# Layer 0's second dense layer goes through DRAM in 26 of 32 graphs, under new planner constants

## The chip, the cores and the metric

The kernel runs on one NeuronCore of a Trainium2 chip. The metric is device time in microseconds for one execution of the whole program, as the median of several runs. Five engines work side by side, each on its own queue of instructions in order: PE multiplies matrices and writes its results into eight banks of PSUM; DVE (VectorE) and ACT (ScalarE) work element by element and are the ones that read the banks; POOL (GpSimd) computes a few powers here; SP (SyncE) issues the transfers, which 16 DMA engines carry out.

## The reference

32 graphs, each with 512 nodes of 256 features and a weighted 512x512 adjacency, pass four layers. Every layer adds its result to its input and normalises each node over the 256 features.

```
x = ln(x + relu(((1+eps)*x + adj@x) @ W1 + b1) @ W2 + b2)          # layer 0, 256 -> 512 -> 256
x = ln(x + prelu(adj @ (x @ W.T + b)))                              # layer 1
h = ln'(x); x = ln(x + x + relu((adj@h)@W_rel + b_rel + h@W_root))  # layer 2
x = ln(x + silu(rms((eps*x + adj@x) @ W1 + b1)) @ W2 + b2)          # layer 3, 256 -> 1024 -> 256
```

Here `ln` is the plain layer norm, `ln'` the one with gain and offset, `rms` a norm over the 1024 hidden values. Everything is float32.

## The kernel before, in words

**Layout.** Within a graph, the 512 nodes are cut into four chunks of 128 (`NC = 4`); a tensor "by token" has the nodes on the 128 partitions, one "by feature" has the features there. All matrix products are made by a scheme of seven products for a 2x2 block product (`seven`, line 851): sums of blocks are formed first on DVE (`left_sums`, `right_sums`, `dense_sums`), seven smaller products go through three banks, and each result is taken out of its bank by a copy or an add.

**Layer 0's second dense layer** (in `layer0`): the hidden tensor h1 is by feature, the result must be by token, to be added to x. In the kernel before, `dense_add` (line 1072) does it in every graph. It uses h1's blocks as the stationary operand and W2's blocks (`A2_0`, 128 columns wide) as the moving one, so its matmuls are 128 columns wide, and the result is by token at once; `take` adds each bank to x on DVE. The bias row b2 has been added to x before (`plus_row`, two DVE adds of 128x512, with a broadcast load by `passing`).

**The other way**, `dense_turned` (line 1097), is used by layer 3 in graphs 1 to 28. It keeps the weights stationary and streams 256 columns of hidden values. The result yT is by feature, four of its evictions are made by ACT, which adds the bias at the same time (`act(..., bias=...)`), and it then has to be turned over: two DVE transposes turn every 32x32 square, and `spread_squares` (line 1277) moves the squares to their places by four stores to a DRAM tile and two loads back. `add_turned` adds the two halves to x on DVE and calls the half of the norm that follows. The DRAM tiles come from a ring of ten (`corners`), which layer 2's `gather_squares` uses as well.

**Which way** is decided by `turns(layer)` (line 1050) from the table `TURN` (line 140): `TURN[0] = (99, 0)` means never.

**Order of the work.** Nothing is issued in the order of the source. Every instruction is entered into a plan (`Plan`, line 286) with its modelled duration and its dependencies. `Plan.order` (line 484) then simulates the engines, picks at each step the op of lowest rank that can start, assigns rooms (35 buffers of 128x1024 in SBUF) and banks, and writes the order out. The rank of an op is its graph times a period, plus a shift of that graph (`SHIFT`), plus how late it may be (`needs`). Up to five graphs are in flight (`FLIGHT = 5`). Constants tell the planner what things cost: `LOAD`, `CORNER`, `TURNED` and the like are (time on the wire, time after it) of transfers, `SPARE` is a margin added to every landing, `HAND` the hand-over between engines, `YIELD` a penalty that keeps DVE from ops that ACT could do, `GENTLE` and `AHEAD` how early loads and ops of later graphs may start. An op with two ways, such as `copy` (line 743) or `Norm.put` (line 1215), goes to the engine that the planner finds sooner free.

**Ends.** The program begins with nine matmuls on zeros (line 1524) while the first loads come in. In the last two graphs (`HALVES = 2`) layer 3 uses `NormOnVector`: for each half of the nodes, once its `dense_add` is complete, DVE takes `bn_stats` of each chunk of 256 features and `bn_aggr` of it, and `finish` scales and stores that half.

```
def turns(layer):
    return TURN[layer][0] < plan.graph < B - TURN[layer][1]
...
if turn:
    add_turned(x, dense_turned(right, A2_0, b2c_0), norm.half)
else:
    dense_add(x, right, A2_0, norm.half)
```

Of the kernel before, what the change touches and what calls it, by code (L numbers as in the profile page):

```python
# [13 lines left out]
ALU = mybir.AluOpType  # L14

P = 128
# [5 lines left out]
def span(ap):  # L22

    n = 1
    for d in ap.shape[1:]:
        n *= d
    return n
# [5 lines left out]
def matmul_time(n):  # L33
    return (0.224 if n <= 128 else 0.432 * n / 256), 0.163
# [6 lines left out]
def vector_time(n):  # L41
    return 0.07 + n * 0.00104, 0.055 if n <= 256 else 0.08
# [7 lines left out]
def stats_time(n):  # L50
    return 0.095 + n * 0.00092, 0.082
# [22 lines left out]

SPARE = 1.2


KEEP = 0.4  # L80
# [3 lines left out]
    return 0.1 + kbytes / 450, 1.0  # L84


LOAD, LOAD_X, BLOCK = (0.86, 1.8), (0.67, 1.4), (0.3, 0.66)
KEPT, BACK = (0.31, 0.5), (0.33, 0.94)
CORNER, PIECES = (0.43, 0.84), (0.61, 1.09)
TURNED, QUARTER = (0.75, 1.05), (0.59, 1.05)  # L90
LINE, SPREAD, RESULT = (0.22, 0.1), (1.45, 0.83), (0.66, 1.1)

GENTLE = 3.5
LOADS = 2

HAND = dict(tensor=0.12, vector=0.09, scalar=0.09, gpsimd=0.14, sync=0.1)
WEIGHTS, AGAIN = 0.09, 0.09


# [13 lines left out]
SOON = 0.03  # L115


YIELD = 0.8

# [2 lines left out]

RULES = [(37, 1.65, 19, 0.9)]

SHIFT = {-1: -26, 0: 12, 1: 3, 2: 2, 5: -1, 7: 1, 14: -1, 29: -7, 30: -16, 31: 4}
HALVES = 2
AHEAD, LAST = 50.0, 500.0
TURN = {0:(99,0),2:(99,0),3:(0,3)}
ROWS = 1
ONE = 1
PLAIN = 0
# [148 lines left out]
class Plan:  # L286
# [191 lines left out]
    def best(self):  # L478


        rule = min(RULES, key=lambda rule: self.order(*rule)[0])
        return self.order(*rule)[1]

    def order(self, period, pace, last, near):
# [28 lines left out]
        while can_start:  # L513
# [52 lines left out]
            for i in can_start:  # L566
# [9 lines left out]
                if op.gentle:  # L576
                    wait = max(wait, wire - GENTLE)
                at = {
                    e: max(free[e] + BEFORE * (op.crosses and not crossed), wait, ready[i][e], port[e] if op.port else 0.0) for e in op.ways
                }  # L580
                way = min(
                    at, key=lambda e: at[e] + sum(op.ways[e][0]) + YIELD * (op.yields and op.graph < B - PLAIN and e == "vector")
                )
# [30 lines left out]
            if op.wire:  # L614
                wire = max(wire, t + ADVANCE) + op.wire
                end = wire + op.late + SPARE + LOADS * op.gentle
                if engine == "sync":
# [11 lines left out]
            for n, result, more in op.then:  # L629
                behind[n] -= 1  # L630
                for e in ready[n]:
                    if e != engine or e != "tensor" and result:
                        ready[n][e] = max(ready[n][e], end + HAND[e] + more)
                if not behind[n]:
# [12 lines left out]
def tile_gnn_stack(ctx: ExitStack, tc: tile.TileContext, a: dict, out: bass.AP):  # L647
# [26 lines left out]
    B, N, D = a["x"].shape  # L674
    NC = N // P
# [5 lines left out]
    HC = NC // 2  # L681
# [8 lines left out]
    plan = Plan(nc, FLIGHT)  # L690
# [31 lines left out]
    def vector(method, n, *args, **kw):  # L722
        return "vector", method, vector_time(n), args, kw
# [2 lines left out]
        columns = sum(k in ("scale", "bias") and not isinstance(v, float) for k, v in kw.items())  # L726
        return "scalar", "activation", times(n, columns), (x,), dict(func=func, **kw)

    def mm(o, lhsT, rhs, first, last):
        kw = dict(start=first, stop=last, skip_group_check=True)  # L730
        way = "tensor", "matmul", matmul_time(span(rhs)), (lhsT, rhs), kw
        plan.do(o, way, ordered=o.room)

    def flip(o, x):
# [20 lines left out]
    def ts(o, x, s1, s2, op0, op1=None):  # L755
        kw = dict(op0=op0) if op1 is None else dict(op0=op0, op1=op1)
        plan.do(o, vector("tensor_scalar", span(o), x, s1, s2, **kw))
# [22 lines left out]
    def small(*shape):  # L780
        return Part(Room(smalls)).shaped(*shape)
# [13 lines left out]
    def half(t, h):  # L795
        return t[:, h * HC : (h + 1) * HC]

    class Wide:


        def __init__(self, n):
            self.n = n
            self.rooms = [room(2, N) for _ in range(n // 2)]
# [245 lines left out]

    def turns(layer):  # L1050

        return TURN[layer][0] < plan.graph < B - TURN[layer][1]

    def halves(x):

# [13 lines left out]
                right.setdefault(m, []).extend(x[:, e] for e in range(n))  # L1069
        return right  # L1070

    def dense_add(x, right, left, done, kind="add"):


        def block(i, j):
            return x[:, j * HC : (j + 1) * HC, i * P : (i + 1) * P]

        def product(m, ps, first):
            n = len(right[m])
            for k in range(n):  # L1080
                for i in range(HC):
                    mm(
                        ps[:, i, :], right[m][k][:, i], left[m][:, k, :],
                        first and i == 0 and k == 0, k == n - 1,
                    )

        def take(ps, i, j):
            add(block(i, j), ps, block(i, j))

        def put(ps, i, j, more):  # L1090
            take(ps, i, j)
            if i == 1:
                done(j)

        seven(kind, partial(bank, HC, P), product, take, put)

# [73 lines left out]
    class Norm:  # L1170
# [33 lines left out]
        def finish(self, h, m, plus, place):  # L1204

            mine = slice(h * HC, (h + 1) * HC)
            ve, rstd, shift = self.ve[:, mine], self.rstd[:, mine], self.shift[:, mine]
            ts(ve, self.squares[:, mine], m / self.n, plus, ALU.mult, ALU.add)
            inv_sqrt(rstd, ve)
            mul(shift, self.less[:, mine], rstd)  # L1210
            for c in range(h * HC, (h + 1) * HC):
                self.put(c, self.r, rstd[:, c % HC : c % HC + 1], shift[:, c % HC : c % HC + 1])
            plan.move(place, half(self.r, h), RESULT, into=f"out{plan.graph}{h}")

        def put(self, c, y, scale, shift):
            r = self.r[:, c, :]
            plan.do(
                y[:, c, :],
                vector(
                    "tensor_scalar", D, r, self.less[:, c : c + 1], scale, op0=ALU.add, op1=ALU.mult  # L1220
                ),
                scalar(AF.Identity, D, r, scale=scale, bias=shift),
            )

# [9 lines left out]
    class NormOnVector(Norm):  # L1234


        def half(self, h):
            means = self.few.then(lambda v: v[:, 0 : 2 * NC].rearrange("p (c i) -> p c i", i=2))
            for c in range(h * HC, (h + 1) * HC):
                st = self.few[:, 8 + 6 * (c % HC) : 14 + 6 * (c % HC)]  # L1240
                plan.do(st, ("vector", "bn_stats", stats_time(D), (self.r[:, c, :],), {}))
                plan.do(means[:, c, :], ("vector", "bn_aggr", stats_time(6), (st,), {}))
            mine = slice(h * HC, (h + 1) * HC)
            ts(self.less[:, mine], means[:, mine, 0], -1.0, None, ALU.mult)
            self.squares, self.n = means[:, :, 1], 1
# [84 lines left out]
    def passing(name):  # L1330

        t = short(N)[:, 0:D]
        plan.move(t, a[name].partition_broadcast(P), D / 2)
        return t

    def plus_row(x, r):
# [138 lines left out]
    def layer3(x, adjacency, b):  # L1475

        aT = aggregate(x, adjacency)
        turn = turns(3)
        if not turn:
            plus_row(x, passing("L3_gnn_b2"))  # L1480
        hT, acc = Wide(FC3), short(N)

        def squares(f):
            sq = room(2, N)
            act(sq, hT.pair(f), AF.Square)
            if f == 0:
                add(acc, sq[:, 0, :], sq[:, 1, :])
            else:
                add(acc, acc, sq[:, 0, :])
                add(acc, acc, sq[:, 1, :])  # L1490

        dense_feat(aT, A1_3, b1_3, hT, squares)
        pr = everywhere(column_sums(acc), (1.0 / HID3, RMS_EPS, ALU.mult, ALU.add))
        right = {}
        for q in range(0, FH, 2):
            for f in (q, q + 1, FH + q, FH + q + 1):
                mul(hT.chunk(f), hT.chunk(f), pr)
                act(hT.chunk(f), hT.chunk(f), AF.Silu, scale=w_3[:, f : f + 1])
            for m, t in dense_sums([halves(hT.pair(q))], [halves(hT.pair(FH + q))]).items():
                right[m] = right.get(m, []) + t  # L1500
        norm = (NormOnVector if b == 0 or b >= B - HALVES else Norm)(x)
        place = out[b].rearrange("(p c) d -> p c d", c=NC)
        if b < B - HALVES:
            if turn:
                add_turned(x, dense_turned(right, A2_3, b2c_3), norm.half)
            else:
                dense_add(x, right, A2_3, norm.half)
            norm.scales((1.0, LN_EPS))
            y = norm.scaled()
            for h in range(2):  # L1510
                plan.move(half(place, h), half(y, h), RESULT, into=f"out{b}{h}", gentle=b < B - 4)
        else:

            def done(h):
                norm.half(h)
                norm.finish(h, 1.0, LN_EPS, half(place, h))

            dense_add(x, right, A2_3, done)

    plan.graph = -1
    idle, zeros = bank(D), scraps[0]
    for _ in range(9):
        mm(idle, zeros[:, 0:P], zeros, True, True)
    eps0 = row("L0_gnn_eps")
    one_eps0 = constant("one_eps0", [P, 1])
    ts(one_eps0, eps0, 1.0, None, ALU.add)
# [4 lines left out]
    x = load_x(0)  # L1533
# [14 lines left out]
    x = layer0(x, adjacency)  # L1548
# [9 lines left out]
    h = layer1(x, adjacency)  # L1558
# [9 lines left out]
    A2_3 = weight_sums("A2_3", *blocks_of(W2_3[:, 0:FH], W2_3[:, FH:]))  # L1568
    layer3(layer2(*h, adjacency), adjacency, 0)
    for b in range(1, B):  # L1570
        plan.graph = b
        x, adjacency = load_x(b), Adjacency(b)
        h = layer1(layer0(x, adjacency), adjacency)
# [45 lines left out]
```

## Time and profile before

| what | value |
|---|---|
| median of 3 runs | 2274.05 us (2273.98 to 2274.63) |
| the profiled execution | 2273.29 us, its span 2271.5 us |
| PE busy | 2260.4 us, 12806 matmul records |
| DVE busy | 2128.1 us (94%) |
| ACT busy | 1807.5 us (80%) |
| mean granted TensorE clock | 0.999 |
| moved by DMA | 172.00 MB, queue q1 26.3% of 16 engines' span |

The span runs from the first instruction to the last; the time of an execution holds a little around it. Each float32 matmul of the source stands as two records in the profile. Records of matmuls overlap their neighbours, so a busy PE is not yet a PE at its peak: the step from one start to the next tells what a matmul costs. Names are those of the program without buffer numbers: `room` is any of the SBUF buffers, `ps` a bank of PSUM, `few` a small buffer, `corner` a DRAM tile of the turning, `A` the sums of weight blocks. As one helper issues everything, nearly all instructions have the same line, and groups are told apart by their names and shapes. "Idle before, releaser" is the time for which an engine rested ahead of an instruction, and what ended the rest.

### The profile page before, as it was taken

What the parts mean: (1) busy time and instruction counts of PE and PEld (TensorE: products, weight loads), DVE (VectorE), ACT (ScalarE), POOL (GpSimd) and SP (SyncE); (2) the same over time, 40 slices, a digit from 0 to 9 for tenths busy, and PEclk for the clock granted to TensorE, in tenths of its full rate; (3) what the DMA queues carried; (4) which work ended last, traced back from release to release, by engine and by line L of the source; (5) the groups of instructions that cost most, each with busy time, mean ns of one, the idle gap of its engine ahead of it and who ended that gap; (6) DMA issues with size and microseconds to landing.
All of it is one profiled execution on the core that took longest, in us unless ns stands there. A gap on an engine that the chain in (4) does not pass through costs nothing.

```text
span 2271.5 us, 39581 instructions
## 1 busy us (share of the span) xinstructions
PE 2260.4 (100%) x12806; PEld 2041.0 (90%) x12806; DVE 2128.1 (94%) x5458; ACT 1807.5 (80%) x4981; POOL 243.5 (11%) x168
## 2 busy tenths in 40 slices
PE   9999999999999999999999999999999999999998
PEld 8889988999989999989999899998999989989888
DVE  8999999999999999989999999999999999999898
ACT  4877778787788787887788887879787788778686
POOL 0100110101011110111011010110111011101011
PEclk9999999999999999999999999999999999999999
DMA  7201331323332233322332313331231322232201
GB/s 220 62 17 34 87 96 42 101 58 93 84 77 54 75 92 89 93 54 67 85 90 61 100 44 90 89 93 51 73 117 52 88 75 53 77 91 48 75 22 59
DMA packets 261790, 172.00 MB, mean 76 GB/s; under 512 B 143824, under 2 KB 213456, under 8 KB 261584
## 3 DMA queue, kind: packets, MB, share of 16 engines
q1 hardware_dynamic: 261584, 169.49, 26.3%
q8 instruction: 101, 1.65, 0.3%
q14 instruction: 105, 0.86, 0.1%
HBM read 114.05 MB, written 55.37 MB: 75 GB/s over the span
## 4 chain that ended last, share of the span: by engine, by line
PE 94%; DVE 4%; DMA 1%; ACT 1%; issue 0%; SPq 0%; POOL 0%; POOLq 0%; ACTq 0%; DVEq 0%
PE ps L371 94%; DVE room L371 3%; ACT room L371 1%; DMA line<-few 0%; DVE few L371 0%; DVE few L396 0%; DMA room<-in_L_gnn_b_dram 0%; DMA room<-line 0%; DMA room<-in_adj_dram 0%; DVE A L371 0%; ACT scrap L371 0%; SPq L418 0%; DVE L_gnn_W L371 0%; DVE L_gnn_W_root L371 0%; POOL few L371 0%
## 5 line engine op out<-in xcount | busy, mean ns | idle before, releaser
L371 PE MATMUL ps<-room,room 128*128 128x256 f32 (+1 forms) x3572 | 915.4, 381 | 0.3 <-DVE room L371 0.2
L371 DVE TENSOR_TENSOR room<-room,room 128x512 f32<-128x512 f32 (+1 forms) x1550 | 878.9, 592 | 13.4 <-ACT room L371 8.8
L371 PEld LDWEIGHTS ps<-room,room 128*128 128x128 f32 x3572 | 635.6, 190 | 74.0 <-issue 3.1
L371 PE MATMUL ps<-room,L_gnn_W 128*128 128x256 f32 x2432 | 650.4, 380 | 0.9 <-DVE pause L1580 0.7
L371 DVE TENSOR_TENSOR room<-ps,room 128x256 f32<-128x256 f32 (+1 forms) x1198 | 549.7, 478 | 62.0 <-PE ps L371 53.2
L371 PEld LDWEIGHTS ps<-room,L_gnn_W 128*128 128x128 f32 x2432 | 445.5, 190 | 57.1 <-ACT room L371 1.6
L371 PE MATMUL ps<-room,A 128*128 128x256 f32 x1824 | 482.3, 379 | 0.0
L371 POOL TENSOR_TENSOR few<-few,mhalf 128x4 f32<-128x4 f32 (+3 forms) x162 | 242.8, 1503 | 2023.2 <-DVE few L371 1309.1
L371 ACT ACTIVATE room<-ps,L_gnn_b_c 128x256 f32<-128x256 f32 x880 | 359.0, 473 | 69.1 <-PE ps L371 67.6
L371 PEld LDWEIGHTS ps<-room,A 128*128 128x128 f32 x1824 | 340.3, 190 | 44.1 <-DVE room L371 0.5
L371 ACT ACTIVATE room<-room,few 128x256 f32<-128x256 f32 x561 | 297.6, 596 | 88.0 <-DVE few L371 87.4
L371 DVE TENSOR_TENSOR room<-room 128x256 f32<-128x256 f32 (+1 forms) x702 | 337.6, 487 | 12.3 <-ACT room L371 9.3
L371 PE MATMUL ps<-A,room 128*128 128x128 f32 x2112 | 308.5, 275 | 1.3 <-DVE room L371 0.6
L371 PEld LDWEIGHTS ps<-A,room 128*128 128x128 f32 x2112 | 290.5, 191 | 16.9 <-DVE room L371 1.9
L371 PEld LDWEIGHTS ps<-L_gnn_W,room 128*128 128x128 f32 x1792 | 267.0, 191 | 20.2 <-DVE room L371 1.1
L371 PE MATMUL ps<-L_gnn_W,room 128*128 128x128 f32 x1792 | 280.0, 275 | 0.5 <-DVE room L371 0.5
L371 ACT ACTIVATE room<-room 128x1024 f32<-128x1024 f32 (+1 forms) x256 | 241.1, 954 | 48.2 <-DVE room L371 35.9
L371 ACT ACTIVATE scrap<-room,few 128x256 f32<-128x256 f32 x500 | 250.1, 502 | 33.6 <-DVE few L371 30.7
L371 ACT ACTIVATE scrap<-room 128x256 f32<-128x256 f32 x500 | 203.5, 408 | 81.7 <-DVE room L371 80.0
L371 ACT ACTIVATE room<-ps 128x256 f32<-128x256 f32 x516 | 190.5, 376 | 83.8 <-PE ps L371 81.4
L371 ACT ACTIVATE room<-room,L_gnn_rms_weight_c 128x512 f32<-128x512 f32 x256 | 172.3, 714 | 13.9 <-DVE room L371 13.5
L371 ACT ACTIVATE ps<-ps 128x256 f32<-128x256 f32 x252 | 93.1, 371 | 39.1 <-PE ps L371 28.5
(62 smaller groups left out, 1263.7 us busy)
## 6 DMA issues: line engine op xcount, KB each, us to landing
room<-in_adj_dram SPq DMA_DIRECT2D x128, 256.0 KB, 4.6
corner<-room SPq DMA_DIRECT2D x232, 128.0 KB, 2.7
room<-in_x_dram SPq DMA_DIRECT2D x64, 256.0 KB, 5.1
out_dram<-room SPq DMA_DIRECT2D x64, 256.0 KB, 2.2
room<-corner SPq DMA_DIRECT2D x120, 128.0 KB, 2.8
room<-corner SPq DMA_DIRECT2D x56, 256.0 KB, 2.8
room<-in_adj_dram SPq DMA_DIRECT2D x128, 64.0 KB, 1.9
diagonal<-room SPq DMA_DIRECT2D x62, 128.0 KB, 1.8
```

The lines of the kernel that those rows point to most:

```text
L371: getattr(getattr(self.nc, engine), method)(to, *(put(x) for x in args), **kw)
```

## The change

Layer 0 takes the turned way in graphs 3 to 28. The planner's constants are replaced. Six matmuls on zeros stand at the start instead of nine, and they are planned at their slow speed. In the last two graphs `NormInQuarters` takes the statistics of the first 128 features of a chunk as soon as the first block of a half is added (`begun`), and those of the other 128 at the end; the two scalings of a half go one to DVE and one to ACT instead of to the engine that the planner picks.

```diff
-SPARE = 1.2
+SPARE = 0.7
...
-LOAD, LOAD_X, BLOCK = (0.86, 1.8), (0.67, 1.4), (0.3, 0.66)
+LOAD, LOAD_X, BLOCK = (1.0, 1.7), (0.75, 1.6), (0.3, 0.66)
 KEPT, BACK = (0.31, 0.5), (0.33, 0.94)
-CORNER, PIECES = (0.43, 0.84), (0.61, 1.09)
-TURNED, QUARTER = (0.75, 1.05), (0.59, 1.05)
-LINE, SPREAD, RESULT = (0.22, 0.1), (1.45, 0.83), (0.66, 1.1)
-GENTLE = 3.5
+CORNER, PIECES = (0.46, 0.86), (0.61, 1.09)
+TURNED, QUARTER = (0.75, 1.05), (0.65, 1.02)
+LINE, SPREAD, RESULT = (0.22, 0.1), (1.45, 0.83), (1.0, 0.5)
+PASSING = 0.5, 1.6
+GENTLE = 3.2
...
-HAND = dict(tensor=0.12, vector=0.09, scalar=0.09, gpsimd=0.14, sync=0.1)
+HAND = dict(tensor=0.15, vector=0.12, scalar=0.12, gpsimd=0.17, sync=0.13)
...
-YIELD = 0.8
+YIELD = 1.1
...
-RULES = [(37, 1.65, 19, 0.9)]
-SHIFT = {-1: -26, 0: 12, 1: 3, 2: 2, 5: -1, 7: 1, 14: -1, 29: -7, 30: -16, 31: 4}
+RULES = [(36, 1.7, 12, 0.7)]
+SHIFT = {-1: -25, 0: 12, 1: 3, 2: 2, 4: 3, 27: -6, 28: -6, 29: -6, 30: -5, 31: 14}
 HALVES = 2
-AHEAD, LAST = 50.0, 500.0
-TURN = {0:(99,0),2:(99,0),3:(0,3)}
+AHEAD, LAST = 89.0, 500.0
+TURN = {0:(2,3),2:(99,0),3:(0,3)}
...
     def turns(layer):
-        return TURN[layer][0] < plan.graph < B - TURN[layer][1]
+        first, last, *each = TURN[layer]
+        return first < plan.graph < B - last and plan.graph % (each or [1])[0] == 0
...
             for c in range(h * HC, (h + 1) * HC):
-                self.put(c, self.r, rstd[:, c % HC : c % HC + 1], shift[:, c % HC : c % HC + 1])
+                i = c % HC
+                plan.do(
+                    self.r[:, c, :],
+                    self.ways(self.r[:, c, :], self.less[:, c : c + 1], rstd[:, i : i + 1], shift[:, i : i + 1])[i],
+                )
...
+    class NormInQuarters(NormOnVector):
...
+        def quarter(self, h, i=0):
+            for c in range(h * HC, (h + 1) * HC):
+                st = self.part(c)[:, 6 * i : 6 * i + 6]
+                r = self.r[:, c, i * P : (i + 1) * P]
+                plan.do(st, ("vector", "bn_stats", stats_time(P), (r,), {}))
+
+        def half(self, h):
+            self.quarter(h, 1)
+            means = self.few.then(lambda v: v[:, 0 : 2 * NC].rearrange("p (c i) -> p c i", i=2))
+            for c in range(h * HC, (h + 1) * HC):
+                plan.do(means[:, c, :], ("vector", "bn_aggr", stats_time(12), (self.part(c),), {}))
...
     def passing(name):
-        plan.move(t, a[name].partition_broadcast(P), D / 2)
+        plan.move(t, a[name].partition_broadcast(P), PASSING)
...
-            dense_add(x, right, A2_3, done)
+            dense_add(x, right, A2_3, done, begun=norm.quarter)
...
-    for _ in range(9):
-        mm(idle, zeros[:, 0:P], zeros, True, True)
+    for _ in range(6):
+        mm(idle, zeros[:, 0:P], zeros, True, True, (0.86, 0.163))
```

More of the change, by code (lines that the diff above doesn't have):

```diff
@@ L727, in scalar, with mm @@
         return "scalar", "activation", times(n, columns), (x,), dict(func=func, **kw)
-    def mm(o, lhsT, rhs, first, last):
+    def mm(o, lhsT, rhs, first, last, times=None):
         kw = dict(start=first, stop=last, skip_group_check=True)
-        way = "tensor", "matmul", matmul_time(span(rhs)), (lhsT, rhs), kw
+        way = "tensor", "matmul", times or matmul_time(span(rhs)), (lhsT, rhs), kw
         plan.do(o, way, ordered=o.room)
@@ L1070, in dense_sums, with dense_add @@
         return right
-    def dense_add(x, right, left, done, kind="add"):
+    def dense_add(x, right, left, done, kind="add", begun=None):
         def block(i, j):
@@ L1093, in put @@
                 done(j)
+            elif begun:
+                begun(j)
         seven(kind, partial(bank, HC, P), product, take, put)
@@ L1211, in finish, with ways @@
             for c in range(h * HC, (h + 1) * HC):
-                self.put(c, self.r, rstd[:, c % HC : c % HC + 1], shift[:, c % HC : c % HC + 1])
+                i = c % HC
[3 more added lines that the diff above has]
+                )
             plan.move(place, half(self.r, h), RESULT, into=f"out{plan.graph}{h}")
         def put(self, c, y, scale, shift):
[L1216 to L1221, printed above, removed]
+            plan.do(y[:, c, :], *self.ways(self.r[:, c, :], self.less[:, c : c + 1], scale, shift))
+        def ways(self, r, less, scale, shift):
+            return (
+                vector("tensor_scalar", D, r, less, scale, op0=ALU.add, op1=ALU.mult),
                 scalar(AF.Identity, D, r, scale=scale, bias=shift),
@@ L1242, in half, with __init__, part @@
                 plan.do(means[:, c, :], ("vector", "bn_aggr", stats_time(6), (st,), {}))
+            mine = slice(h * HC, (h + 1) * HC)
+            ts(self.less[:, mine], means[:, mine, 0], -1.0, None, ALU.mult)
+            self.squares, self.n = means[:, :, 1], 1
+    class NormInQuarters(NormOnVector):
+        def __init__(self, r):
+            super().__init__(r)
+            self.parts = small(64)
+        def part(self, c):
+            return self.parts[:, 12 * c : 12 * c + 12]
+        def quarter(self, h, i=0):
[8 more added lines that the diff above has]
+                plan.do(means[:, c, :], ("vector", "bn_aggr", stats_time(12), (self.part(c),), {}))
             mine = slice(h * HC, (h + 1) * HC)
@@ L1500, in layer3 @@
                 right[m] = right.get(m, []) + t
-        norm = (NormOnVector if b == 0 or b >= B - HALVES else Norm)(x)
+        norm = (NormInQuarters if b >= B - HALVES else NormOnVector if b == 0 else Norm)(x)
         place = out[b].rearrange("(p c) d -> p c d", c=NC)
```

## The prediction

> **What bounds the kernel now.** I read the page's head first, then the chain that ended last, then the windows, then single matmul rows. The page:
>
> ```profile
> span 2271.5 us, 39581 instructions
> PE 2260.4 (100%) x12806; PEld 2041.0 (90%) x12806; DVE 2128.1 (94%) x5458; ACT 1807.5 (80%) x4981; POOL 243.5 (11%) x168
> q1 hardware_dynamic: 261584, 169.49, 26.3%
> ```
>
> PE (the matrix engine) never rests by this view and DVE nearly never. A busy PE is not yet a PE at its peak, so the chain decides who is waited for:
>
> ```profile
> 1248.16 6.64 DMA line<-few
> 1254.81 3.25 DMA room<-line
> ...
> 95.32 189.34 PE ps L371 x1124
> 284.69 962.70 PE ps L371 x5374
> ...
> 1259.59 687.97 PE ps L371 x3828
> ```
>
> From 95 to 1247 and from 1259 to 1947 us the chain is matmul after matmul: nothing else ends last. The break at 1248 is one transfer through DRAM that landed late. The windows say the same of the middle, and show who is next:
>
> ```profile
> 20.00:60.00 40.00, 39.77 (x244) 35.77 (x245) 39.59 (x114) 24.17 (x72) 2.03 (x2) 1.00 0.60 181
> 284.00:1247.00 963.00, 962.97 (x5377) 870.79 (x5376) 907.87 (x2313) 781.57 (x2156) 106.32 (x68) 1.00 0.27 77
> 1260.00:1975.00 715.00, 714.97 (x4006) 645.96 (x4005) 673.40 (x1715) 573.93 (x1588) 76.23 (x50) 1.00 0.27 77
> ```
>
> Columns: length, busy PE, PEld, DVE, ACT, POOL, granted clock, DMA share, GB/s. In the middle DVE has 6% to spare, ACT 19%, DMA 73%; in the first 60 us DVE is as full as PE. What a matmul really costs is the step between starts, read from PE's own timeline:
>
> ```profile
> 2199.70 5.35 PE L371 MATMUL ps<-room,A 128*128 128x256 f32 x24
> 2208.50 3.73 PE L371 MATMUL ps<-L_gnn_W,room 128*128 128x128 f32 x32
> ```
>
> With 0.38 us for the last record (0.275 for the narrow kind; mean times of the groups), the step is (5.35 - 0.38)/23 = 0.216 us at 256 columns and (3.73 - 0.275)/31 = 0.112 at 128. A matmul of the source makes two records. By the groups of equal shape there are 7838 records of 256 columns, 4952 of 128 and 16 of 512 (0.429 each, from 7.03 us for 16): 1693.0 + 554.6 + 6.9 = 2254.5 us. Only 17.0 us of the span is not matmul at full step: 1.2 before the first, about 7 after the last begins, and about 9 of pauses, the slow clock of the first microseconds among them. So the time falls if matmul steps go, or rises if pauses come.
>
> **The change, part by part.**
>
> *Layer 0's second dense layer, graphs 3 to 28 (26 graphs).* PE: `dense_add` makes 7 products x 2 x 2 = 28 matmuls of 128 columns, 56 records, 56 x 0.112 = 6.27 us. `dense_turned` makes 14 of 256 columns, 28 records, 28 x 0.216 = 6.05 us. Gain 0.224 us a graph, 5.8 us in all, and on the path wherever PE is the chain, which is where these graphs lie.
>
> Here a rule gives another size. The Trainium skill, "TensorE: Matmul & The Clock Gate", section "Back-to-back issue gap", lists 134 cycles for 128 columns and 262 for 256. Two narrow ones would then lose 6 of 268 cycles against one wide one, 2.2%, where the rows above give 3.6%; by the page the gain would be an estimated 3.6 us instead of 5.8 and the result near 2269. I keep the rows.
>
> DVE loses, a graph: two adds of the bias row (128x512, 0.680 each) and six adds out of the banks (128x256, 0.414), 3.84 us. It gains two of those adds, two stream transposes (0.698) and two adds of the returned half (0.680), 3.58. Net -0.26 us of a 71 us period, so its share stays at 94%: worth nothing while PE leads. ACT gains four evictions with bias (0.473), +1.9 us, from 56.3 (mean of eleven 71 us windows) to 58.2 of 71: hidden in its 19%. Were that cover gone it would cost up to 1.9 x 26 = 49 us, but ACT would have to be full first. The higher penalty for DVE in the planner (YIELD 0.8 to 1.1) pushes a few of the 79 scalings that DVE took (0.405 us) to ACT; hidden as well.
>
> Transfers and SP: four stores and two loads more a graph, and one broadcast load of 128 KB less.
>
> ```profile
> corner<-room SPq DMA_DIRECT2D x232, 128.0 KB, 2.7
> out_dram<-room SPq DMA_DIRECT2D x64, 256.0 KB, 2.2
> room<-corner SPq DMA_DIRECT2D x56, 256.0 KB, 2.8
> room<-in_L_gnn_b_dram SPq DMA_DIRECT2D x36, 128.0 KB, 4.6
> ```
>
> (The last columns are the size and the median us from issue to landing.) Issue on SP costs 4 x 0.56 + 2 x 0.41 - 0.35 = 2.7 us a graph. Bytes: 26 x 0.9 MB = 24 on 172, so the DMA share goes from 26% to about 30%. The way from the last product to the normalisation grows by 0.5 (eviction) + 1.4 (transposes) + about 2.2 (four issues) + 2.7 + 0.8 + 2.8 + 0.7 - 0.4 (the add it had), about 10.7 us. It is hidden: five graphs are in flight, so one has some 340 us from load to output (loads of graph 5 at 253 us, just behind the store of graph 0 at 245), and PE takes other graphs' products meanwhile. Its load parks on SP until its stores land; the next graphs' adjacency and x queue behind. SP waited for such stores 61.0 us over 69 times, 2.3 at most, and PE did not wait.
>
> [...]
>
> *Planner constants* (SPARE, LOAD, CORNER, HAND, GENTLE, RULES, SHIFT, AHEAD, PASSING): no instruction, only another order. The title's longer times are only half of it: SPARE falls by 0.5, so a corner store is planned to land 1.0 + 0.46 + 0.86 + 0.7 = 3.0 us behind its issue where it was 3.5; the row has 2.7, the longest corner transfer 6.8. What the new order does to pauses no row shows. Bounds: -5 us, if most of the pauses after the cold start go; +17, if each of the 26 hops does what the late one at 1248 did (between the starts at 1255.76 and 1261.62 us PE's timeline has 20 records of 256 columns and 8 of 128, 5.22 us at full step, in 5.86: 0.64 lost). Of the 88 hops through DRAM (30 by line, 30 plus 28 by corner) that is the only one on the long chain, so I take 0.
>
> *Six idle matmuls instead of nine.*
>
> ```profile
> 1.18 5.83 PE L371 MATMUL ps<-scrap 128*128 128x256 f32 x18 [1.18 <-DVE scrap L842]
> 4.56 0.29 DVE L371 TENSOR_TENSOR room<-room,loop 128x128 f32<-128x128 f32 x1 [0.37 <-DMA room<-in_adj_dram]
> 6.85 7.03 PE L371 MATMUL ps<-room,room 128*128 128x512 f32 x16
> ```
>
> Six records at the warm step, 1.3 us, end before 6.85. The first block is ready at 4.85 and the first half of x at 1.63 + 3.9 = 5.5, so real work can begin up to 1.2 us sooner. But later blocks wait for their transfers and DVE is full from 20 to 60 us, which the gain has to pass. Bounds 0 and 1.3; I take 0.5.
>
> *Last statistics by quarters, and the last scaling split.*
>
> ```profile
> 2265.13 0.43 DVE L371 BATCH_NORM_STATS2 few<-room 128x6 f32<-128x256 f32 x1
> 2265.69 0.39 DVE L371 BATCH_NORM_STATS2 few<-room 128x6 f32<-128x256 f32 x1
> 2266.34 0.24 DVE L371 TENSOR_SCALAR few<-few 128x2 f32<-128x2 f32 x2
> 2267.51 1.09 ACT L371 ACTIVATE room<-room,few 128x256 f32<-128x256 f32 x2 [0.77 <-DVE few L371]
> ```
>
> Behind the last add, statistics and aggregates alternate for 1.21 us. With half of the columns taken earlier and both aggregates last, I estimate 0.9: gain 0.3, bounds 0 and 0.6 (no shorter than the two aggregates, 0.174 each, and two short statistics). The scaling, two on ACT in 1.09, becomes one on each engine (ACT 0.60 beside DVE 0.41): 0.5. Together 0.8, all of it on the path.
>
> Sum: -5.8 + 0 - 0.5 - 0.8 = -7.1 us. The profiled execution took 2273.29 (its span and 1.8 around it): 2266.2. The median of the runs, 2274.05, lies 0.76 higher; I predict against it: **2267.0**.
>
> **Rivals.**
>
> *The hop comes back late (slower).* Place: layer 1's first product in graphs 3 to 28, waiting for the turned output. Price 0.64 us as behind 1248, 26 times: +16.6, giving 2283.6. It outweighs the gain from 12 late hops (7.1/0.64 = 11.1), and 19 make it measurably slower ((7.1 + 4.5)/0.64 = 18.1). For it: SPARE is 0.5 us smaller, and the ten corner tiles now turn three times a graph, so layer 0 of graph g writes the tile that layer 3 of graph g-4 read. Against: SP's timeline has layer 3 of graph 6 storing at 617.01 and loading back at 619.82, and graph 10 getting its diagonals back, before its dense layers, only at 633.99; and one late hop in 88.
>
> *The gain is eaten (no change).* Pauses of 0.1 to 0.45 us a graph, because DVE at 94% meets two transposes in one burst: 2269.5 to 2278.6, middle 2274. For: DVE's share. Against: DVE has less to do than before.
>
> *More than the sum.* The order loses pauses as well, up to 5 us: 2262. For: about 1.4 us of DVE-led pauses at 2072 and 2205 (0.55 and 0.90, from the starts of the records) and more before 95 lie where SHIFT was rewritten. Against: the full DVE there is not lightened.
>
> **How the numbers follow.** Main case 0.56 (2264.5 to 2269.5), more than the sum 0.14 (2262 to 2264.5), no change 0.15, slower 0.15. Two tenths of a per cent, 4.5 us, is about what a measurement here can tell from no change. Faster 0.70, same 0.15, slower 0.15. The range 2263 to 2276 leaves out the low end (0.03), the top of "no change" (0.02) and the slower case.
>
> **What would show it.** 3496 records of 128 columns and 8560 of 256; 336 corner stores (232 + 104) and 108 whole-size loads; the bias load 10 times instead of 36; the middle still a chain of PE without a break; real matmuls beginning near 5.7 us; about 0.8 us less behind the last matmul. The prediction is wrong if the windows of the middle show PE short by 0.3 us a graph with room or corner as the releaser, or if head and tail pauses grow.

## The result, and the profile after

The changed kernel takes 2293.23 us (median of 4 runs, 2288.82 to 2295.80) against 2274.02 for the kernel before in the same comparison: a ratio of 1.008, 95% interval 1.0068 to 1.0092. It was forecast at 2267.0, in a range from 2263 to 2276. It is slower, by 19 us, and its runs spread over 7 us where those of the kernel before stay within 1.3.

The page's head of the changed kernel (profiled execution 2295.8 us):

```profile
span 2294.0 us, 38435 instructions
PE 2270.7 (99%) x12072; PEld 2015.0 (88%) x12072; DVE 2120.8 (92%) x5419; ACT 1843.8 (80%) x5100; POOL 242.1 (11%) x168
q1 hardware_dynamic: 280304, 193.35, 30.4%
```

The work is what the prediction said: 734 matmul records fewer, DVE a little less, ACT a little more, DMA at 30.4%. The trace has 8560 records of 256 columns, 3496 of 128 and 16 of 512. At full step (0.216, 0.112, 0.429 us) they need 2247.4 us, 7.1 less than before. What is not matmul step has grown from 17.0 us to 2294.0 - 2247.4 = 46.6. **The gain is there, and pauses of 29.6 us stand against it.** (The profiled execution is the slowest of the four; by the medians the pauses are some 3 us fewer.)

The chain that ended last, which was one long run of PE before, is now cut in many places:

```profile
720.93 129.41 PE ps L372 x662
850.37 0.77 DVE room L372 x2
...
854.77 1.81 ACT room L372 x4
856.85 4.20 ACT room L372 x10
862.21 128.95 PE ps L372 x662
...
1103.75 6.92 DMA room<-in_adj_dram
1110.68 3.28 DMA room<-in_x_dram
1114.55 1.02 DVE room L372 x2
1116.03 17.55 PE ps L372 x102
...
1247.99 8.32 DMA room<-corner
```

Two kinds of cut are to be seen. At 850 to 862 a chain of DVE and ACT work ends last, 14 ACT ops in a row; the same piece comes back at 709, 991 and on, every second graph. At 1103 and 1248 a transfer ends last. The chain puts the stretch at 1103 down to an adjacency load and an x load, but DVE's timeline names another transfer, and the view of the transfers issued from 1104.7 to 1106.8 us tells how long it took:

```profile
1113.34 1.29 DVE L372 TENSOR_TENSOR room<-room 128x512 f32<-128x512 f32 x2 [1.75 <-DMA room<-corner]
...
room<-corner SPq DMA_DIRECT2D x4, 128.0 KB, 6.8
```

DVE stood 1.75 us for four corner loads of 128 KB, and PE then for DVE. Loads of that size are layer 2's; those of the turned way have 256 KB. They had been issued right behind two adjacency loads. At 1248 the corner load of 8.32 us is again one of four of layer 2. The windows of the middle:

```profile
284.00:1247.00 963.00, 959.39 (x4948) 850.05 (x4947) 894.13 (x2259) 799.30 (x2218) 101.62 (x68) 1.00 0.32 88
1260.00:1975.00 715.00, 712.41 (x3692) 630.67 (x3691) 665.69 (x1683) 583.75 (x1623) 76.27 (x51) 1.00 0.32 89
```

In the first of them DVE is less full than before (93% for 94%) and ACT a little fuller (83% for 81%); PE rests although on the mean both have time to spare. The wide windows also hide bursts. This is the view of the transfers issued from 1244 to 1258 us (queue, packets, MB and share; then size and us to landing):

```profile
q1 hardware_dynamic: 1945, 3.18, 83.3%
...
room<-in_adj_dram SPq DMA_DIRECT2D x4, 256.0 KB, 8.3
...
room<-corner SPq DMA_DIRECT2D x4, 128.0 KB, 8.3
```

The mean of 30% is 83% here, and an adjacency load takes 8.3 us where the median of the kernel before was 4.6 (over the whole changed kernel it is 5.1).

### The profile page after: what moved, and what is told of

It reads as the page before. It is cut to its first block, busy times and chain, and to the rows that moved or that the text cites. A ratio compares the mean times of both kernels' runs of the same rounds, so it can differ in the third digit from the quotient of the medians.

```text
span 2294.0 us, 38435 instructions
## 1 busy us (share of the span) xinstructions
PE 2270.7 (99%) x12072; PEld 2015.0 (88%) x12072; DVE 2120.8 (92%) x5419; ACT 1843.8 (80%) x5100; POOL 242.1 (11%) x168
## 3 DMA queue, kind: packets, MB, share of 16 engines
q1 hardware_dynamic: 280304, 193.35, 30.4%
## 4 chain that ended last, share of the span: by engine, by line
PE 78%; DVE 9%; ACT 7%; DMA 4%; issue 1%; SPq 1%; DVEq 0%; POOLq 0%; POOL 0%; ACTq 0%
PE ps L372 78%; DVE room L372 8%; ACT room L372 6%; DMA room<-corner 1%; DMA room<-in_adj_dram 1%; ACT scrap L372 1%; DVE few L372 1%; SPq L419 1%; DMA room<-in_x_dram 0%; DMA diagonal<-room 0%; ACT ps L372 0%; DMA corner<-room 0%; DVE few L397 0%; DMA L_gnn_W_root<-in_L_gnn_W_root_dram 0%; DMA L_gnn_b_c<-in_L_gnn_b_dram 0%
## 5 line engine op out<-in xcount | busy, mean ns | idle before, releaser
L372 PE MATMUL ps<-room,L_gnn_W 128*128 128x256 f32 x2848 | 779.1, 381 | 3.9 <-DVE room L372 2.5
L372 PEld LDWEIGHTS ps<-room,L_gnn_W 128*128 128x128 f32 x2848 | 522.3, 190 | 83.7 <-ACT room L372 13.2
L372 PE MATMUL ps<-room,A 128*128 128x256 f32 x2136 | 569.7, 379 | 1.3 <-ACT room L372 1.2
L372 ACT ACTIVATE room<-ps,L_gnn_b_c 128x256 f32<-128x256 f32 x984 | 417.6, 472 | 85.8 <-PE ps L372 70.8
L372 PEld LDWEIGHTS ps<-room,A 128*128 128x128 f32 x2136 | 400.9, 190 | 55.0 <-ACT room L372 1.7
L372 ACT ACTIVATE room<-room,few 128x256 f32<-128x256 f32 x576 | 304.3, 598 | 40.5 <-DVE few L372 40.4
L372 ACT ACTIVATE room<-ps 128x256 f32<-128x256 f32 (+1 forms) x514 | 192.5, 381 | 91.3 <-PE ps L372 88.8
L372 ACT ACTIVATE room<-room 128x1024 f32<-128x1024 f32 (+1 forms) x256 | 241.1, 950 | 19.2 <-DVE room L372 10.6
L372 PEld LDWEIGHTS ps<-A,room 128*128 128x128 f32 x1488 | 205.6, 191 | 14.4 <-DVE room L372 3.4
L372 PE MATMUL ps<-A,room 128*128 128x128 f32 x1488 | 217.1, 276 | 0.8 <-DVE room L372 0.8
L372 PEld LDWEIGHTS ps<-L_gnn_W,room 128*128 128x128 f32 x960 | 137.5, 191 | 11.6 <-DVE room L372 1.8
L372 PE MATMUL ps<-L_gnn_W,room 128*128 128x128 f32 x960 | 144.2, 275 | 1.9 <-DVE room L372 1.2
```

What stands on the lines that cost most here:

```text
L372: getattr(getattr(self.nc, engine), method)(to, *(put(x) for x in args), **kw)
```

## The experiments

Two theories. **Lateness:** transfers land later than the order allows for, because of the new hop and the smaller margin. **Order:** the pauses stand in the order that the planner wrote. For the second, the planner's own arithmetic can be asked: it gives every op a start, and the gaps between its planned matmuls add up to planned pauses. The kernel before has 12.4 us of them, the changed one 22.7. By the plan alone the last matmul ends at 2266.9 us before and at 2272.7 after: the planner itself puts the changed kernel behind. Against these I set what the trace has: the span less the matmul records at full step, 17.0 us before.

### Layer 0's hop cut short

```diff
-plan.move(places[a], of[a * Q : (a + 1) * Q], CORNER, into=name)
+plan.move(places[a], of[a * Q : (a + 1) * Q], CORNER, into=name, cut=16 * short)   # 16 partitions, 1 KB each
...
-plan.move(to.whole(N * DC)[:, mine], via[:, mine], TURNED, outof=...)
+plan.move(to.whole(N * DC)[:, mine], via[:, mine], TURNED, outof=..., cut=16 * short)  # 16 of 128 partitions
```

> The changed kernel with its order of instructions kept exactly, but layer 0's corner transfers in graphs 3 to 28 carry 16 of 128 partitions (stores of 16 KB, loads of 32 KB; layer 0's result is therefore not the reference's). Lateness theory (the hop through DRAM lands later than the order allows for, and PE waits for it or for loads beside it): most of the 17 us that PE lost beyond the planned order goes, time 2276 to 2284. Order theory (the pauses stand in the order written out, whatever the transfers do): within 3 us of the changed kernel, 2290 to 2296.

Measured 2284.80 us (2283.48 to 2286.44), ratio 1.0045, 1.003 to 1.006. That is 8.4 us below the changed kernel, with the same instructions in the same order and only fewer bytes, and just above the band that the lateness theory gave. The chain between 1095 and 1120 us, where transfers had ended last, is now

```profile
1094.79 25.22 PE ps L372 x140
```

so the bytes of layer 0's hop had been delaying layer 2's loads; the hop's own result was not what was waited for there. Elsewhere it was. What DVE waited for corner loads (us in total, times, longest), in the changed kernel and here:

```profile
DVE room L372 <- DMA room<-corner: 17.2, 21, 2.7
DVE room L372 <- DMA room<-corner: 3.2, 4, 2.1
```

The kernel before has 0.2 us, once. Told apart wait by wait in the trace of the changed kernel, layer 0's own halves have some 7.5 us of this in 16 waits and layer 2's loads about as much in 10. Relative to its planned start, PE's last matmul fell 13.4 us behind over the run in the changed kernel and 1.1 here, where the kernel before gains 3.6 us on its plan. But the time not spent in matmul steps is still 2281.7 - 2247.4 = 34.3 us, twice that of the kernel before. The ACT piece of every second graph stays as well:

```profile
852.72 4.20 ACT room L372 x10
```

Lateness is a part; 17.3 of the 29.6 us are left, by the medians 10.1 of 19.2.

### Output stores cut short

```diff
-plan.move(half(place, h), half(y, h), RESULT, into=f"out{b}{h}", gentle=b < B - 4)
+plan.move(half(place, h), half(y, h), RESULT, into=f"out{b}{h}", gentle=b < B - 4, cut=16)
```

> The changed kernel, same order, but the output stores of graphs 0 to 29 carry 16 of 128 partitions (the output is not written whole). Lateness theory in the form of crowding (output stores, the next graph's loads and corner loads leave in one burst and share the DMA engines): time falls by 4 to 10 us, to 2283 to 2289. If the hop alone is late, or by the order theory: 2290 to 2296.

Measured 2289.99 us (2287.69 to 2290.61), 3.2 us below the changed kernel and at the edge of what either theory gave. The runs of the two overlap (the changed kernel's begin at 2288.82), so whether these bytes matter is not shown; those of layer 0's hop do.

### Only the turn

```diff
-TURN = {0:(99,0),2:(99,0),3:(0,3)}
+TURN = {0:(2,3),2:(99,0),3:(0,3)}
```

> The kernel before with layer 0 turned in graphs 3 to 28 and nothing else changed (planner constants, idle matmuls and statistics as before, so 0.5 us more margin on every landing). If the smaller margin caused the loss: 2268 to 2276. Order theory (the constants are fitted to one set of operations, and any other set gets a poor order): the order that the planner writes for it holds 100 us of PE pauses by its own arithmetic against 12 for the kernel before, so 2335 to 2365.

Measured 2350.73 us, one run. With the old margin of 1.2 and all other constants as before, the order gets far worse: 100.3 us of planned pauses, and 2349.0 - 2248.7 = 100.3 us not in matmul steps on the chip. Along the middle PE kept within 3 us of that plan, so nothing there was late. A third of it is one pause near the end, which stands in the plan too, with 41.7 us at 2197:

```profile
2190.00 7.54 PE L371 MATMUL ps<-room,L_gnn_W 128*128 128x256 f32 x24 [33.33 <-ACT room L371]
```

A loss thus needs no smaller margin; the old constants give a poor order for the new operations, near the end above all.

### Only the edits at the ends

```diff
-    for _ in range(9):
-        mm(idle, zeros[:, 0:P], zeros, True, True)
+    for _ in range(6):
+        mm(idle, zeros[:, 0:P], zeros, True, True, (0.86, 0.163))
+(statistics by quarters and the split last scaling, as in the change)
```

> The kernel before with only the edits at the two ends: six idle matmuls planned at 0.86 us, statistics by quarters, split last scaling. Priced in the prediction at -1.3 us, 2272 to 2273. Order theory: the new planned time of the idle matmuls shifts the first choices of the planner, and its order then holds 31 us of pauses instead of 12: 2288 to 2294.

Measured 2293.12 us (2292.35 to 2294.14), ratio 1.0082, 1.0068 to 1.0096. Edits that remove work, without any turning, cost as much as the whole change. PE's timeline shows where (what released it stands in the brackets):

```profile
142.32 1.12 PE L371 MATMUL ps<-ident,few 128*128 128x128 f32 x4 [7.99 <-POOL few L371]
144.98 3.79 PE L371 MATMUL ps<-L_gnn_W,room 128*128 128x128 f32 x16 [1.53 <-ACT room L371]
```

PE stood 8 us for the power that graph 0's layer 3 needs (`everywhere`), because the order had put nothing else for it there. Behind the pause the matmuls themselves are slow, (3.79 - 0.275)/15 = 0.234 us a step at 128 columns instead of 0.112, and the granted clock (the 0.50) is half:

```profile
140.00:149.00 9.00, 4.90 (x20) 4.21 (x20) 6.56 (x17) 3.51 (x6) 1.01 (x1) 0.50 0.01 2
```

The planned pauses rose from 12.4 to 30.7 us, and 2291.5 - 2253.2 = 38.3 are there on the chip.

### The same edits in the usual order

```diff
-        mm(idle, zeros[:, 0:P], zeros, True, True, (0.86, 0.163))
+        mm(idle, zeros[:, 0:P], zeros, True, True)
```

> The same edits at the ends, but the six idle matmuls planned at the usual time, which leaves the planned order of everything up to the last two graphs as it was. If the prices of the prediction hold once the order is the same: 2272 to 2273.5 (0.8 at the end and 0 to 1 at the start). Order theory agrees; it would be against it if this one too lost more than 3 us.

Measured 2272.76 us (2271.74 to 2273.49, 11 runs) against 2274.38; ratio 0.9992, 0.9983 to 1.0001. Planned at the usual 0.432 us, the six idle matmuls leave the first choices of the planner as they were. One number in the planner's cost of an idle matmul is worth 20 us. With the order kept, the ends give what they were priced at, within the noise. PE's row of the first real work, and the last of ACT:

```profile
5.51 7.23 PE L371 MATMUL ps<-room,room 128*128 128x512 f32 x16
```

```profile
2266.86 0.60 ACT L371 ACTIVATE room<-room,few 128x256 f32<-128x256 f32 x1 [1.39 <-DVE few L371]
```

Real work begins at 5.51 us where it was 6.85, of which some 0.5 us reaches the end, and one scaling of 0.60 us stands on ACT where two took 1.09. The span is 1.1 us shorter. This version beats the changed kernel clearly and the kernel before by about 1.6 us, at the limit of what can be told (the interval still holds 1).

### Layer 0 turned in ten graphs, old constants

```diff
-TURN = {0:(99,0),2:(99,0),3:(0,3)}
+TURN = {0:(13,8),2:(99,0),3:(0,3)}
(on top of the version above)
```

> The end edits in the usual order and layer 0 turned in graphs 14 to 23 only, with the old constants and the old margin of 1.2; up to graph 13 the planned order is that of the kernel before. By the prediction's price of 0.224 us a graph: 2.2 us below the run with the end edits alone, 2270 to 2271. By the order theory (the planner's order for this has 8 us more pauses, all of them from graph 13 on, and its last op 5.7 us later): 2277 to 2280. If the margin of 1.2 is enough, PE stays with that plan; if turned hops are late even so, 2281 or more.

Measured 2278.24 us (2277.44 to 2279.04), ratio 1.002, 1.001 to 1.0029: as the planned order said, and 6.3 us worse than the version without the turn (each against the kernel before of its own comparison: +4.7 and -1.6). The ten graphs were chosen by the planner's own account, as a wide range whose order has few planned pauses. Windows ahead of the turned graphs and over them:

```profile
284.00:923.00 639.00, 638.69 (x3562) 577.83 (x3562) 604.36 (x1554) 518.36 (x1435) 71.13 (x46) 1.00 0.28 78
1065.00:1775.00 710.00, 706.24 (x3712) 627.90 (x3711) 666.72 (x1698) 577.11 (x1603) 76.27 (x50) 1.00 0.30 87
```

The kernel before has PE at 638.97 and 709.80 us in the same windows: the pauses come only where layer 0 is turned. There are 249 records fewer in the second window, and PE still loses 3.6 us more. Nothing is late here: planned pauses rise by 9.2 us, measured ones by 26.1 - 17.0 = 9.1.

### A smaller margin, no turn

```diff
-SPARE = 1.2
+SPARE = 0.8
```

> The kernel before (no layer 0 turned) with SPARE 0.8 instead of 1.2, nothing else. The planner writes another order, with 49 us of PE pauses by its own arithmetic and its last op at 2308.6. If the small margin alone makes transfers late: PE falls 5 to 15 us behind that plan, 2312 to 2325. If it takes the turned hops to make them late: the chip stays with the plan as in the kernel before (within 4 us, ahead rather than behind), 2303 to 2311.

Measured 2314.13 us (2312.87 to 2314.89), ratio 1.0174. Again most of it is the order (36.4 us more planned pauses); the chip adds about 5 us (58.1 - 17.0 = 41.1). What came late there was not looked up.

All of these beside each other, in us more than the kernel before. Where the six idle matmuls are planned at 0.86 us instead of 0.432 (the ends alone and both rows of the changed kernel), the 6 x 0.43 = 2.6 us are counted with the planned pauses, since the measured column takes every matmul at full step:

| run | planned pauses | time not in matmul steps | difference |
|---|---|---|---|
| ends, same order | +1.3 | +0.2 | -1.1 |
| turn in ten graphs | +9.2 | +9.1 | -0.1 |
| ends alone | +20.9 | +21.3 | +0.4 |
| margin 0.8 | +36.4 | +41.1 | +4.7 |
| turn only | +87.9 | +83.3 | -4.6 |
| the changed kernel | +12.9 | +29.6 | +16.7 |
| the changed kernel, hop cut short | +12.9 | +17.3 | +4.4 |

The order that is written out tells the time within 5 us in all rows but that of the changed kernel. There the chip adds 16.7 us to it, and 12.3 of these go when the hop carries an eighth of its bytes (8.4 by the medians: the profiled executions are the slowest of four there and the fastest of four here). Among the matmuls planned between 284 and 1975 us, where most of the turned graphs lie, the plan has 2.2 us of pauses before and 9.4 after; the chip has 0.8 before, 22.3 after and 12.0 with the hop cut short.

### The transfers by themselves

Five runs put layer 0's six transfers a graph on the kernel before, with nothing that uses their result, behind layer 0's last op of graphs 3 to 28. The order is fixed, so they stand on SP where no slot was planned for them.

```diff
+for a in range(P // Q):
+    nc.sync.dma_start(places[a], W2_3[a * Q : (a + 1) * Q, 0:NC])       # 4 stores of 128 KB
+for h in range(2):
+    nc.sync.dma_start(sink, traffic[:, h * SINK : (h + 1) * SINK])      # 2 loads of 256 KB, behind the stores
```

> The kernel before, same order, with the added transfers alone: behind layer 0's last op of graphs 3 to 28, four stores of 128 KB and two loads of 256 KB through a DRAM tile that nothing else uses (the loads wait for the stores, as in the turned way). Crowding: 2280 or more, since the traffic is what delays other transfers. Order theory, or lateness of the hop itself: 2273 to 2277, since nothing waits for these transfers.

Measured 2330.57 us (2326.64 to 2334.53), ratio 1.0246: 56 us, far more than the change itself lost. It is crowding's number, but in this run bytes and waits come together; the next runs part them.

```diff
-    nc.sync.dma_start(sink, traffic[:, h * SINK : (h + 1) * SINK])
+    nc.sync.dma_start(sink, <half h of graph 31's x>)
```

> As the run with the added transfers on the kernel before, the same bytes, the same six issues on SP at the same places, but the two loads read an input instead of the tile just stored, so they wait for no store. If the 56 us there came of bytes on the shared DMA engines or of six more issues: again 2320 or more. If SP stood at a load until its stores had landed, with later transfers parked behind it: 2274 to 2285.

Measured 2324.87 us (2318.80 to 2330.98). By its expectation bytes or issues did it, but the run had a flaw: both loads fill one tile, so the second waits on SP for the first. SP's timeline shows it:

```profile
770.04 1.93 SPq L1389 DMA_DIRECT2D traffic<-L_gnn_W  x4
772.02 4.98 SPq L1392 DMA_DIRECT2D sink<-in_x_dram  x2
777.09 0.38 SPq L419 DMA_DIRECT2D line<-few  x1
```

SP stood 4.98 us at the two loads. The small `line` store, which layer 3 needs for its norm, was parked behind them; in the chain PE starts again only after that line is back. Two more runs, one with two sink tiles and so no wait, one with the first run's waits but stores of 16 KB and loads of 32 KB:

```diff
-    nc.sync.dma_start(sink, <half h of graph 31's x>)
+    nc.sync.dma_start(sinks[h], <half h of graph 31's x>)
```

> The added transfers on the kernel before once more, full bytes, but now without any wait among themselves: the loads read an input and go to two tiles, where in the run before the second load still waited on SP for the first to land. If SP standing at a wait, with the real transfers parked behind it, is what cost 50 us: 2275 to 2285. If the bytes or the six issues are: 2310 or more.

```diff
-    nc.sync.dma_start(places[a], W2_3[a * Q : (a + 1) * Q, 0:NC])
+    nc.sync.dma_start(places[a][0:16, 0:1], W2_3[a * Q : a * Q + 16, 0:1])
-    nc.sync.dma_start(sink, traffic[:, h * SINK : (h + 1) * SINK])
+    nc.sync.dma_start(sink[0:16], traffic[0:16, h * SINK : (h + 1) * SINK])
```

> The added transfers on the kernel before with their waits kept as in the first such run (loads behind stores, second load behind the first) but 16 KB stores and 32 KB loads. Parking on SP: a landing takes some 2 us whatever its size, so 2300 to 2325. Bytes on the DMA engines: 2275 to 2282.

Measured 2292.97 us (2292.40 to 2296.93) and 2293.86 (2291.68 to 2295.84), against 2273.56: neither expectation alone held, each half keeps some 20 us. The last run takes both away:

> The added transfers on the kernel before with both taken away: no waits among them and 16 KB stores and 32 KB loads, so that only the six issues a graph are left on SP. If bytes made the 19 us of the run without waits and waits the 20 us of the run with few bytes: 2274 to 2278 here. If the six issue slots on SP are what both had in common: 2288 to 2295.

Measured 2277.31 us (2275.60 to 2279.18) against 2274.78. SP now passes in 0.88 us, and the line goes out at once:

```profile
756.55 1.85 SPq L1389 DMA_DIRECT2D traffic<-L_gnn_W  x4
758.44 0.88 SPq L1392 DMA_DIRECT2D sink<-in_x_dram  x2
759.42 0.67 SPq L419 DMA_DIRECT2D line<-few  x1
```

| us above the kernel before | few bytes | full bytes |
|---|---|---|
| no waits on SP | 2.5 | 19.4 |
| waits on SP | 20.3 | 55.9 |

Over 26 graphs, six more issues cost 0.1 us a graph, bytes 0.65 more, waits 0.7 more, and all together 2.15: 18.7 us in all above the sum. Two things in the traces go with it. A wait lasts longer when the bytes are many: SP stood 57.9 + 40.4 us for the added loads and stores in the run with both, 34.1 + 23.4 in that with few bytes (stores landed in 2.9 us for 2.1 in the median). And the clock falls. From PE's timeline in the run with both, behind a pause of 3.30 us, and the window over it:

```profile
429.16 0.91 PE L372 MATMUL ps<-room,L_gnn_W 128*128 128x256 f32 x2 [3.30 <-ACT room L372]
429.86 2.83 PE L372 MATMUL ps<-room,room 128*128 128x256 f32 x6
...
433.15 1.46 PE L372 MATMUL ps<-room,L_gnn_W 128*128 128x256 f32 x6
```

```profile
429.50:432.90 3.40, 3.40 (x10) 2.53 (x9) 3.04 (x9) 2.33 (x8) 1.01 (x1) 0.50 0.08 22
```

At a granted clock of 0.50, six records take 2.83 us; three microseconds later six of the same width take 1.46. There are nine such stretches before the last matmul, of 3.4 or 6.8 us, each soon behind a pause of 2 us or more, and their doubled steps add up to 15 us of the 56. The run with waits and few bytes has two (3.4 us), the two runs without waits none. So pauses that are long enough cost more than themselves; how long is not settled here, since one of 3.1 us at 1943 brought no such stretch. (In the middle windows of the kernel before and of the changed one the clock stays at 1.00.) These are prices for an order that does not know of the transfers. The changed kernel's order does, and loses less.

## Why the prediction was wrong

- **"PE: gain 0.224 us a graph, 5.8 us in all."** Right. The counts of records are those foretold, 3496 and 8560, and with the idle matmuls the matmul work fell by 7.1 us. The Trainium skill's page "TensorE: Matmul & The Clock Gate", section "Back-to-back issue gap", lists cycles that make an estimated 2.2% between two narrow matmuls and a wide one; the rows of the trace had 3.6%, and no run here shows the smaller figure.
- **"Planner constants: no instruction, only another order ... I take 0."** This is the step that failed. Its bounds were -5 and +17; it measured +29.6 us: 12.9 stand in the new order as planned, 16.7 come of the chip falling behind that plan, 12.3 of these by the hop's bytes. The upper bound took only late hops and had no place for an order with pauses of its own, which the planner's arithmetic shows without a run. I had costed every moved instruction and taken the quality of the order as given, when it hangs on one set of constants. With these the planner's choices leave 12 us of pauses in the kernel before. Four changes tried around it fell off that point: an idle matmul's planned time +19 us, a margin of 0.8 us +40, the turn alone +76, the turn in ten graphs 6 us more than without it. The changed kernel's constants leave 22.7 us.
- **"It is hidden: five graphs are in flight."** Half right. With the margin of 1.2 (ten graphs) PE stayed with its plan. With 0.7 and bursts at 83% of the DMA engines the hop's bytes made layer 0's and layer 2's loads late, 8.4 us in the medians. I had read a mean share of 26% rising to 30% as room.
- **"In 88 hops one was late, so I take 0."** The rate came from an order with 0.5 us more margin and other bursts, and did not carry over.
- **The slower rival** had the right sign and a part of the mechanism, at 2283.6. Its place was half right: DVE did wait for layer 0's turned output, some 7.5 us in 16 waits, but as long for layer 2's loads, which the hop's bytes delayed; how much of each reached PE is not shown. And it left out the 12.9 us of the order.
- **"The gain is eaten", by DVE.** No: DVE is at 92%, lower than before.
- **The ends: -0.5 and -0.8 us.** Right where the order is kept: 0.5 and 0.7 (from the last matmul's start to the end of the span, 6.48 us for 7.15). In the changed kernel real work begins at 6.24 us, and the 0.3 us gained behind the last matmul do not matter.

What stays open is how much of the order's 12.9 us goes with turning as such and how much with the choice of the constants, and what the 4.4 us are that the chip still adds with the hop cut short. The one order here for all 26 graphs with the old margin, the turn alone, is far worse than the kernel before; that is no proof that there is no better one.

## What to carry to other kernels

When a planner or a hand-made order stands between the source and the queues, removing work is not yet removing time: price the new order first, by the planner's own account of its pauses, and change one thing while the order is held fixed. A mean share of the DMA engines says nothing of bursts; look at the stretch in which the next inputs, the outputs and the new transfers leave together. And on an in-order issue queue a transfer that must wait for another is paid by whoever stands behind it.

## What was not expected of the hardware

Bytes and waits on the issuing queue cost more together than their sum: 19.4 and 20.3 us alone, 55.9 together, for the same 156 transfers, in part because PE ran at half its clock behind the longer pauses, 15 us in all. And transfers of other layers suffer too: four corner loads of layer 2 landed in 6.8 us in a burst with layer 0's hop, and in 4.8 in the same burst with the hop cut short; an adjacency load of 256 KB went from a median of 4.6 us to 8.3.
